# Four cross-attention layers in one kernel: other turns for the third layer's own attention, other shares and another order for its closings and for the rows added back

## The chip, the core and the metric

The kernel runs on one core of one Trainium2 chip. The core has five engines with a queue each: TensorE (PE, with its weight loads shown apart as PEld), VectorE (DVE), ScalarE (ACT), GpSimd (POOL) and SyncE (SP, which here only issues transfers). The metric is the time of one execution on the device in microseconds; the kernel before takes 1442.94 us in the median of three runs (1436.54, 1442.94 and 1444.49).

## What is computed

Four layers follow each other on `x` (16 batches of 56 rows, width 256). All of them look at the same context `ctx` (16 batches of 1500 rows, width 128). Cut to what matters:

```python
def reference(x, ctx, pos, mask_ctx, token_types, ...):
    x = L0(x, ctx)                       # one attention to ctx, a gate, an rms norm
    x = L13(x, ctx, mask_ctx, L1)
    x = L2(x, ctx, token_types, pos)
    x = L13(x, ctx, mask_ctx, L3)
    return x

def L13(x, ctx, mask, w):                # 16 heads of 64
    q = layernorm(x) @ Wq / 8
    k, v = split(ctx @ Wkv)
    x = x + tanh(g1) * (softmax(where(mask, q @ k.T, lowest)) @ v) @ Wo
    return x + tanh(g2) * gelu(layernorm(x) @ W1) @ W2

def L2(x, ctx, token_types, pos):        # vm marks the rows of the "v" expert
    h = rms_norm(x)
    q, k, v = split(where(vm, h @ v_qkv, h @ l_qkv))
    a = causal_attention(rotary(q), rotary(k), v)        # within a batch's 56 rows
    x = x + where(vm, a @ v_dense, a @ l_dense)
    x = x + attention(rms_norm(x) @ cq, ctx @ ckv) @ cdense
    m = rms_norm(x)
    return x + where(vm, mlp_v(m), mlp_l(m))
```

In this data the mask of layers L1 and L3 leaves only columns among the last 384 of the context, so the kernel takes its short way for them (`short`): it reads only those 384 columns.

## The kernel before

**Groups and items.** The 16 batches are worked on in four groups of four. A layer and a group make an *item*: item 4·layer + group, from 0 to 15. So items 4 to 7 are layer L1, items 8 to 11 layer L2 and items 12 to 15 layer L3. For each item the program runs an attention to the context as its main line: `att0`, `att13` (which calls `rows` once for a batch) or `att2`. Everything else of the neighbouring items is *side work*, written as Python generators and cut into *turns* by `yield`: `pre13` and `pre2` (norm, queries, and in L2 the layer's own attention with its dense projection) for the next item, `post13` (Wo, norm, W1, W2) for the item before, and `post2` (the experts' products of L2, for two groups together). `beside(k)` strings the side work of item k together; `late()` holds what is spread over items 7 to 12, among it `post2(0)`, `post2(1)` and the adding back of their rows for groups 0 and 1.

**How side work is paced.** The main line asks for turns at fixed places. In `att2` a step is one pair of context chunks of one batch: six steps a batch, 24 an item, numbered 0 to 23 here. Each step issues `weights_pair` (L1441 and L1450 on PE, the exponentials L1455 on ACT, the additions L1467 on POOL), then asks for side work (the *first turn*), then issues the maxima of a later pair (`largest`, L1404 on PE and L1409 on DVE), the sums of an earlier one (`sums_chunk`, L1482), at some steps `shifts` (step 4 of a batch), `own_sums` (step 1), `close_group` (step 2) and the projections of a later batch's keys or values (L1375, L1387), and asks again (the *second turn*). A number behind `yield` is the cost of the turn; `pace(share, kept, most)` adds a share to an account, `line["due"]`, and takes turns while the account lies above a bound (first turn: the item's share, bound -0.8, at most one; second turn: no share, bound 0.6, at most two). A bare `yield` is an empty turn: it ends the asking and takes nothing off the account, which is cut to 3.0. If the first turn did work, the maxima come before the sums, else after them. `SHARES` has one pair of shares for each of the items 8 to 11; the second holds once the next item's `pre` is done. In items 13 to 15 `rows` asks with `step` instead: one turn for each of the seven rows of a batch (two for each of the first two rows of the third and fourth batch), whatever it costs. Where a main line needs the next item's `pre` and it isn't finished, `first` runs the rest of it at once: before step 15 of items 8 to 10, before step 21 of item 11, before the fourth batch in items 12 to 14.

**Who sets the order.** Instructions run in order within an engine's queue. The order of the program is the order of the calls above; a planner at compile time may issue an instruction earlier if the one before it isn't ready by its own account. `behind(made, name, reason)` adds an edge that keeps `made` after the named instruction on the same engine. Transfers issued by SP, ACT and POOL stand in those engines' queues.

**The places that the change touches.**
- `self_attention` in `pre2` (L1304 to L1330): for two pairs of batches `pr` and two halves `e` of the heads, `scores` (PE, then maximum, subtraction on DVE and exponential on ACT), `weights(pr, e)` (DVE: sum L1178, reciprocal L1179, scaling L1180), `turns(pr, e)` (PE: 32 products L1188 that turn the weights, copied by ACT at L302), `sums(pr)` (PE: L1205, then ACT and DVE). After the sums come the two products `ce` with the experts' masks (DVE, L1322) and the dense projection (PE, L1329, in two halves of eight products), the residual (DVE, L1335), and the norm for the attention to the context: squares on ACT (L389), then POOL (L390, the root L320, the scaling L400), transposes on PE (L310).
- `SHARES` (L1354) and `shifts` (L1413 to L1431; its last instruction copies the shifts on DVE, L1430). `line["drained"]` is the name of the last instruction that emptied a bank of `largest` or, in `rows`, of scores.
- `fetch(gi)` (L1675): two indirect transfers on POOL's queue (L1679) that bring a group's rows back from the experts; `take(gi)` (L1687): their addition to `x` on DVE (L1689), kept behind `line["drained"]`, and the first part of L3's norm (DVE L339, L340, L344; POOL: the root L320 and the scaling L354). The transposes of that norm (L310) and the query products (L907) are `pre13`.
- `beside` for item 13 (L1747 to L1758): fetching and adding back of groups 2 and 3, ahead of `pre13` for group 2. `post13` of L3's group 0 follows after that (Wo products L1092, W1 products L1120).
- `late` (L1816 to L1829): the same for groups 0 and 1 after `post2(0)`.

Of the kernel before, what the change touches and what calls it, by code (L numbers as in the profile page):

```python
# [62 lines left out]
def tile_kernel(ctx: ExitStack, tc: tile.TileContext, a, layers=4, groups=NG):  # L63
# [3 lines left out]
    nc = tc.nc  # L67
# [14 lines left out]
    def psum(pool, tag):  # L82
        return pool.tile([128, 512], F32, tag=tag, name=tag)
# [5 lines left out]
    def mm():  # L89
        return psum(ps_s, "sc")  # L90

    def turn():
        return psum(ps_s, "sc")
# [452 lines left out]
    line, memory_w, halves_of, queries, heads_w, cross, held, begun = {}, [], {}, {}, {}, {}, {}, {}  # L546
# [675 lines left out]
    def pre2(gi):  # L1222
# [12 lines left out]
        scores, weights, turns, sums = self_attention(qT, kept, v, cT)  # L1235
# [68 lines left out]
        weights(0, 1)  # L1304
        turns(0, 0)
        yield 1.2
        weights(1, 0)
        turns(0, 1)
        yield 1.2
        weights(1, 1)  # L1310
        sums(0)
        yield 0.7
        turns(1, 0)
        yield 1.2
        turns(1, 1)
# [4 lines left out]
        for n, m in enumerate((vm, nvm)):  # L1320
            mrow = m[:, gi * G : (gi + 1) * G, :].rearrange("p b n -> p (b n)")
            nc.vector.tensor_tensor(  # L1322
                ce[:, n], cT, mrow.unsqueeze(1).to_broadcast([128, 2, T]), ALU.mult
            )
        p = mm()
        for i in range(NT):
            for n in range(2):
# [23 lines left out]

    QH = 4 * N
    PAIRS = NC // 2
    SHARES = (2.1, 1.65), (2.1, 1.1), (2.1, 1.7), (1.9, 1.9)  # L1354

    def spread_queries(b):

# [55 lines left out]
    def shifts(b):  # L1413

        made = cross[b]
        nm = few(8)[: 2 * N]
        nc.vector.tensor_reduce(nm, made["mx"], AX.X, ALU.max, negate=True)
        both = minus[b % 2]
        nc.vector.tensor_copy(both[:, :, 0].bitcast(F32R), nm)
        nc.vector.tensor_tensor(both[:, :, 1], nm, both[:, :, 0], ALU.subtract)  # L1420
        t = turn()
        for n in range(8):
            half, g = divmod(n, 4)
            nc.tensor.matmul(
                t[g * BW : (g + 1) * BW, half * 2 * N : (half + 1) * 2 * N],
                both[:, n, :], ident[: 2 * N, : 2 * N], start=True, stop=True,
                skip_group_check=True,
            )
        shift = small.tile([128, QH], F32R, tag="shift", bufs=2, name="shift")
        nc.vector.tensor_copy(shift, t[:, :QH])  # L1430
        made["shift"] = shift  # L1431

    def weights_pair(b, j):
# [119 lines left out]
    def att2(gi, state, then, ends):  # L1553

        for k in range(G):
            b = gi * G + k
            for j in range(PAIRS):
# [6 lines left out]
                weights_pair(b, j)  # L1564
                full = pace(SHARES[gi][line["behind"]], -0.8, 1)
                last, n = (b, 2 * j - 2) if j else (b - 1, NC - 2)
# [120 lines left out]
    def take(gi, y):  # L1687
        xf = xs[gi].rearrange("p i d -> p (i d)")
        behind(nc.vector.tensor_add(xf, xf, y), line["drained"], "banks go first")  # L1689
        if gi < 3:  # L1690
            begin_layernorm("L3_ln_q_g", gi)

    def program():
# [25 lines left out]
        def beside(k):  # L1719
# [19 lines left out]
            if k:  # L1739
                _, _, _, post, gi = items[k - 1]  # L1740
                follows = line["late"] if third else post(gi, states.get(k - 1))
# [5 lines left out]
            if k == 3 * groups + 1:  # L1747
                while line["stage"] < 5:
                    yield next(line["late"], 0)
                yield  # L1750
                yield
                back = fetch(2), fetch(3)
                for _ in range(7):
                    yield
                take(2, back[0])
                yield
                take(3, back[1])
                yield  # L1758
            if k > groups:
                for work in ahead:  # L1760
                    if isinstance(work, tuple):
# [36 lines left out]
        def late():  # L1798
# [18 lines left out]
            yield  # L1817
            yield
            y = fetch(0)
            for _ in range(4):  # L1820
                yield
            take(0, y)
            line["stage"] += 1
# [50 lines left out]
    t = turn()  # L1874
# [164 lines left out]
```

## Time and profile before

| what | value |
|---|---|
| median of three runs | 1442.94 us |
| the profiled execution, whole | 1437.15 us |
| its span, first to last instruction | 1435.3 us |
| mean granted TensorE clock | 0.986 |
| ACT busy | 744.8 us, 52% |
| DVE busy | 777.7 us, 54% |
| POOL busy | 526.2 us, 37% |
| items 8 to 10, 450 to 915 us: PE busy of 465 us | 453.2 us |
| item 11, 915 to 1072 us: PE busy of 157 us | 148.0 us, clock 0.97 |
| item 13, 1183 to 1247 us: PE busy of 64 us | 58.5 us, clock 0.95 |

The span runs from the first to the last instruction that the profiler recorded; 1.85 us of the execution lie around it. Busy time is the union of an engine's instructions. PE's instructions are pipelined and their ends are modelled, so a PE that counts as busy may still be slow: the granted clock is given beside it. In a timeline, each row is a run of equal instructions on one engine: start, time covered, engine, line, operation, tiles and shapes, their number, and in brackets the idle time of the engine just before them with the instruction that ended it. L302 is a helper for copies on ACT and L310 one for transposes, so these are told apart by their tiles.

### The profile page before, as it was taken

The numbers are of one execution on the slowest core, as the hardware profiler recorded it, in microseconds if no ns is written. First come the engines' busy times: TensorE is split into PE (matmuls) and PEld (weight loads), VectorE is DVE, ScalarE is ACT, GpSimd is POOL, SyncE is SP. The second block draws the span as 40 slices with busy tenths as digits, with TensorE's granted clock in tenths as the row PEclk, the third lists the DMA queues.
The fourth block names the chain that finished last, engine by engine and source line by source line (L and its number), as shares of the span: only waits on it lengthen the run. The fifth ranks groups of instructions, "written<-read, shape, count | busy, mean of one in ns | idle before, by whom it ended". The sixth has DMA issues, their size and how long they took to land.

```text
span 1435.3 us, 32417 instructions
## 1 busy us (share of the span) xinstructions
PE 1357.3 (95%) x13638; PEld 938.2 (65%) x13638; DVE 777.7 (54%) x1794; ACT 744.8 (52%) x1703; POOL 526.2 (37%) x567
## 2 busy tenths in 40 slices
PE   6989999999899999999999999999899998999998
PEld 4667677775656556655555556656467776877776
DVE  4444754647575754467545755455565445455641
ACT  2334866756543547445554544444356565557661
POOL 0011001010101677767767768788743112100000
PEclk9999999999999999999999999999999999999998
DMA  7853224232322021110201022131122343333320
GB/s 270 351 191 126 85 89 145 90 112 65 103 76 81 23 82 52 54 56 24 81 31 43 29 71 68 52 103 56 39 82 94 134 152 101 124 118 123 108 89 10
DMA packets 38808, 135.78 MB, mean 95 GB/s; under 512 B 8605, under 2 KB 18493, under 8 KB 34557
## 3 DMA queue, kind: packets, MB, share of 16 engines
q1 hardware_dynamic: 33901, 119.03, 24.1%
q0 software_dynamic: 2592, 10.85, 2.2%
q10 hardware_dynamic: 2160, 3.74, 0.8%
q8 instruction: 109, 1.79, 0.5%
q14 instruction: 46, 0.38, 0.1%
HBM read 129.01 MB, written 4.59 MB: 93 GB/s over the span
## 4 chain that ended last, share of the span: by engine, by line
PE 75%; DVE 12%; ACT 6%; POOL 3%; DMA 3%; issue 1%; SPq 0%; DVEq 0%; POOLq 0%; ACTq 0%
PE sc L642 9%; PE sc L624 8%; PE sc L1092 7%; PE sc L1404 7%; PE sc L1450 4%; PE o L1482 4%; PE sc L1642 4%; DVE mx L1409 3%; PE sc L907 3%; PE sc L1120 3%; PE sc L1387 3%; PE sc L1441 3%; PE sc L1661 2%; PE sc L1375 2%; POOL all L1467 2%; ACT p L302 2%
## 5 line engine op out<-in xcount | busy, mean ns | idle before, releaser
L1467 POOL TENSOR_TENSOR all<-all,pw 125x448 f32<-125x448 f32 x300 | 341.1, 1149 | 125.8 <-ACT pw L1455 114.7
L1409 DVE TENSOR_REDUCE mx<-sc 112x1 f32<-112x500 f32 x384 | 233.4, 669 | 140.6 <-PE sc L1404 140.5
L1455 ACT ACTIVATE pw<-sc 125x448 f32<-125x448 f32 x384 | 177.7, 550 | 102.8 <-PE sc L1450 100.1
L631 ACT ACTIVATE p<-p,few 128x384 f32<-128x384 f32 x224 | 136.9, 611 | 99.3 <-DVE few L627 98.9
L624 PE MATMUL sc<-ktl,qa 128*128 128x384 f32 x448 | 176.9, 504 | 0.0
L627 DVE CUSTOM_DVE_ANT_0 p<-sc,mkl 128x384 f32<-128x384 f32 x224 | 121.8, 551 | 92.1 <-PE sc L624 87.4
L642 PE MATMUL sc<-p,kvl 32*128 32x224 f32 x2160 | 149.5, 353 | 4.7 <-DVE qa L940 3.3
L642 PEld LDWEIGHTS sc<-p,kvl 32*128 32x128 f32 x2160 | 136.3, 185 | 20.5 <-issue 9.6
L642 PE MATMUL o<-p,kvl 32*128 32x224 f32 x720 | 144.6, 352 | 0.0
L143 POOL TENSOR_SCALAR mkl<-m32l 128x384 bf16<-128x384 uint8 x32 | 16.3, 510 | 314.1 <-DVE few L627 292.5
L642 PEld LDWEIGHTS o<-p,kvl 32*128 32x128 f32 x720 | 130.7, 185 | 0.0
L302 ACT ACTIVATE p<-p,few 128x384 f32<-128x384 f32 x224 | 121.1, 608 | 8.6 <-DVE few L618 7.2
L1404 PE MATMUL sc<-ck,qs 32*112 32x500 f32 x768 | 122.5, 626 | 2.8 <-ACT ck L302 1.4
L661 DVE STREAM_TRANSPOSE p<-p 128x768 f32<-128x768 f32 (+1 forms) x96 | 102.8, 1095 | 28.6 <-ACT p L302 28.4
L624 PEld LDWEIGHTS sc<-ktl,qa 128*128 128x128 f32 x448 | 78.8, 190 | 37.4 <-issue 9.0
L1450 PE MATMUL sc<-qs,ck 32*125 32x224 f32 x1536 | 98.8, 355 | 0.0
L320 POOL TENSOR_TENSOR stat<-stat,half_less 112x2 f32<-112x2 f32 (+1 forms) x33 | 23.1, 700 | 201.8 <-DVE stat L344 162.0
L302 ACT ACTIVATE ot<-sc 128x224 f32<-128x224 f32 x64 | 32.0, 609 | 121.1 <-PE o L642 83.5
L1482 PE MATMUL o<-pw,vc 125*32 125x224 f32 x1536 | 93.0, 359 | 0.0
L1482 PEld LDWEIGHTS o<-pw,vc 125*32 125x32 f32 x1536 | 40.2, 109 | 69.9 <-issue 57.2
L1450 PEld LDWEIGHTS sc<-qs,ck 32*125 32x125 f32 x1536 | 77.4, 183 | 1.1
L302 ACT ACTIVATE vc<-sc 125x512 f32<-125x512 f32 x48 | 28.6, 596 | 82.0 <-PE sc L1387 79.2
(286 smaller groups left out, 2360.7 us busy)
## 6 DMA issues: line engine op xcount, KB each, us to landing
kvl<-in_ctx_last SPq DMA_DIRECT2D x30, 768.0 KB, 4.2
kt<-in_ctxT SPq DMA_DIRECT2D x23, 750.0 KB, 5.0
w<-in_L_W SPq DMA_DIRECT2D x16, 1024.0 KB, 4.8
w<-in_L_Wq SPq DMA_DIRECT2D x8, 1024.0 KB, 5.0
w<-in_L_Wo SPq DMA_DIRECT2D x8, 1024.0 KB, 5.6
ktl<-in_ctxT SPq DMA_DIRECT2D x32, 192.0 KB, 2.5
w<-in_L_v_qkv SPq DMA_DIRECT2D x4, 768.0 KB, 6.8
w<-in_L_l_qkv SPq DMA_DIRECT2D x4, 768.0 KB, 4.1
```

The source lines that it names most:

```text
L302: nc.scalar.activation(out, in_, AF.Copy, scale=scale)
L624: line["scored"] = nc.tensor.matmul(sc[:, :LW], u["q"][:, i * 128 : (i + 1) * 128], u["kt"], start=True, stop=True).ins.name
L627: line["drained"] = nc.vector.tensor_tensor_reduce(u["p"][:, i], sc[:, :LW], u["mask"], 1.0, -LOWEST, ALU.add, ALU.min, mn[:, i : i + 1],) ...
L631: nc.scalar.activation(u["p"][:, i], u["p"][:, i], AF.Exp, bias=mn[:, i : i + 1], scale=-1.0, accum_out=den[:, i : i + 1],)
L642: product = nc.tensor.matmul(o[g][:, : RB * BW], y["kv"][part, j, :], y["p"][part, :, j * BW : (j + 1) * BW], start=j == 0, stop=j == LB - ...
L661: nc.vector.transpose(blocks, blocks)
L1404: nc.tensor.matmul(banks[g][: 2 * N, :SW], made["q"][part, rows], made["k"][part, cols], start=True, stop=True,)
L1409: line["drained"] = nc.vector.tensor_reduce(made["mx"][:, half * 4 + g, s : s + 1], banks[g][: 2 * N, :SW], AX.X, ALU.max).ins.name
L1450: nc.tensor.matmul(banks[g][:CP, c * QH : (c + 1) * QH], made["k"][part, at : at + CP], made["q"][part], start=False, stop=c == 1, skip_gr ...
L1455: line["weighed"] = nc.scalar.activation(p[:, :, g * QH : (g + 1) * QH], banks[g][:CP, : 2 * QH].rearrange("p (c n) -> p c n", c=2), AF.Ex ...
L1467: added = engine.tensor_tensor(made["all"][:, cols], made["all"][:, cols] if j else p[:, 0, cols], p[:, c, cols], ALU.add,)
L1482: nc.tensor.matmul(made["o"][part, :QH], made["v"][:, n, part], p[:, r * QH : (r + 1) * QH], start=n == 0, stop=n + 1 == NC, skip_group_ch ...
```

## The change

The diff touches three places.

In the layer's own attention, `weights(1, 0)` moves behind `turns(0, 1)`, `weights(1, 1)` behind `sums(0)`, and three empty turns are added: before `turns(0, 1)`, before `turns(1, 0)`, and between the products `ce` and the dense projection.

In the closing of L2's attention, the shares of items 10 and 11 grow, `line["drained"]` also names the copy of the shifts, and `late` lets five turns pass in place of four between `fetch(0)` and `take(0)`.

In item 13, the rows of groups 2 and 3 are fetched after four empty turns instead of two; then the program waits until the attention of item 12 is closed and runs five turns of `post13` before `take(2)`, one before `take(3)` and one behind it, where it had seven, one and one empty turns.

```diff
@@ pre2 @@
         weights(0, 1)
         turns(0, 0)
         yield 1.2
-        weights(1, 0)
+        yield
         turns(0, 1)
         yield 1.2
-        weights(1, 1)
+        weights(1, 0)
         sums(0)
         yield 0.7
+        weights(1, 1)
+        yield
         turns(1, 0)
         yield 1.2
         turns(1, 1)
...
                 ce[:, n], cT, mrow.unsqueeze(1).to_broadcast([128, 2, T]), ALU.mult
             )
+        yield
         p = mm()
...
-    SHARES = (2.1, 1.65), (2.1, 1.1), (2.1, 1.7), (1.9, 1.9)
+    SHARES = (2.1, 1.65), (2.1, 1.1), (2.1, 2.0), (2.15, 2.15)
@@ shifts @@
-        nc.vector.tensor_copy(shift, t[:, :QH])
+        line["drained"] = nc.vector.tensor_copy(shift, t[:, :QH]).ins.name
@@ beside @@
             if k == 3 * groups + 1:
                 while line["stage"] < 5:
                     yield next(line["late"], 0)
-                yield
-                yield
+                for _ in range(4):
+                    yield
                 back = fetch(2), fetch(3)
-                for _ in range(7):
+                while line["closed"] < k:
                     yield
+                for _ in range(5):
+                    yield next(follows, 0)
                 take(2, back[0])
-                yield
+                yield next(follows, 0)
                 take(3, back[1])
-                yield
+                yield next(follows, 0)
@@ late @@
             y = fetch(0)
-            for _ in range(4):
+            for _ in range(5):
                 yield
             take(0, y)
```

## The prediction

> **What bounds the kernel now.** I read the page's busy shares first, then the timeline around every long PE wait, then the stretches' clock, then the DMA issues.
>
> ```profile
> PE 1357.3 (95%) x13638; PEld 938.2 (65%) x13638; DVE 777.7 (54%) x1794; ACT 744.8 (52%) x1703; POOL 526.2 (37%) x567
> ...
> L1467 POOL TENSOR_TENSOR all<-all,pw 125x448 f32<-125x448 f32 x300 | 341.1, 1149 | 125.8 <-ACT pw L1455 114.7
> ```
>
> PE is busy for 95% of the span, so only its waits can be won; all matrix products stay as they are. The second line is the next limit: in the third layer's attention to the context POOL adds four times 1149 ns a step, 4.65 us, while a step without side work takes PE 4.5 us (1021.37 to 1025.91 between the starts of two steps).
>
> The timeline of the third layer's item 9 (group 1's attention; start, duration, in brackets PE's idle time and what ended it):
>
> ```profile
> 664.29 1.14 PE L1188 MATMUL sc<-ident,s 120*64 120x56 f32 x32 [1.53 <-DVE s L1180]
> ...
> 684.08 1.98 PE L1329 MATMUL sc<-w,l 128*112 128x256 f32 x8 [1.66 <-DVE l L1322]
> ...
> 693.11 0.19 POOL L390 TENSOR_SCALAR stat<-stat 112x2 f32<-112x2 f32 x1
> ...
> 696.51 0.55 PE L310 MATMUL sc<-ident,xn 112*128 112x112 f32 x4
> ```
>
> PE waits 1.53 us for DVE's second softmax scaling before the second `turns`, and 1.66 us for the two `ce` products before the dense projection. Behind that runs the norm: residual (689.17), POOL from 693.11 to 696.04, and the transposes of L310 without a wait. POOL is free then because the wait delayed the next additions.
>
> The timeline of item 11's end (the last group's attention) and one stretch of it (stretch, length, busy and count of PE, PEld, DVE, ACT, POOL, granted clock, DMA share, GB/s):
>
> ```profile
> 1032.76 1.15 DVE L1689 TENSOR_TENSOR x<-x,back 112x512 f32<-112x512 f32 x1 [0.91 <-DMA back<-made,place]
> ...
> 1035.20 0.97 PE L1424 MATMUL sc<-ident,minus 112*32 112x112 f32 x16 [2.93 <-DVE minus L1420]
> ...
> 1038.37 0.45 PE L310 MATMUL sc<-ident,xn 112*128 112x112 f32 x1 [2.19 <-POOL xn L354]
> ...
> 1039.58 0.82 PE L310 MATMUL sc<-ident,xn 112*128 112x112 f32 x3 [0.76 <-POOL xn L354]
> ```
>
> ```profile
> 1028.00:1043.00 15.00, 8.70 (x93) 5.18 (x86) 7.16 (x16) 3.39 (x8) 13.98 (x14) 0.72 0.06 17
> ```
>
> `take(0)` (1032.76) stands on DVE ahead of the shifts, so PE waits 2.93 us for them, then 2.19 and 0.76 us for POOL's normalised rows. The clock is 0.72 in the stretch, and products stretch with it: eight of L907 take 2.88 us where 1.78 is usual (1050.58).
>
> Item 13 (the fourth layer's second group, L3 in the names):
>
> ```profile
> 1194.55 2.20 PE L624 MATMUL sc<-ktl,qa 128*128 128x384 f32 x6
> ...
> 1196.11 0.08 DVE L627 DVE_READ_ACCUMULATOR2_ANT few<- 128x1 f32 x1
> ...
> 1201.61 0.34 PE L310 MATMUL sc<-ident,xn 112*128 112x112 f32 x1 [4.86 <-POOL xn L354]
> ...
> 1204.42 8.36 PE L907 MATMUL sc<-xT,w 128*128 128x224 f32 x32 [0.60 <-DVE xT L379]
> ```
>
> PE has 4.86 us with nothing to do until the rows fetched for group 2 are added (1196.11) and normalised; L907's 32 products then take 8.36 us.
>
> **The change, part by part.** I counted the turns on paper, with `pace`'s rule, the yields' values and the shares; for the kernel before, this puts `fetch(0)`, `take(0)` and the transposes into steps 14, 16 and 16 of item 11, where the trace has them. The planner may issue an instruction earlier when another isn't ready (L1482 goes ahead of L1441 around the dense products), so the places are good to about half a step.
>
> (a) *The empty turns*, items 8 to 10. Before: step 7's first turn has weights(1,0) and turns(0,1); step 8 weights(1,1), sums(0), then turns(1,0); step 9 turns(1,1), then sums(1), `ce` and half of the dense product; step 10 its other half. After: turns(0,1) in step 7's second turn; weights(1,0) and sums(0), then weights(1,1) in step 8; turns(1,0), then turns(1,1) and sums(1) in step 9; `ce`, then both dense halves in step 10. The norm stays in step 11's first turn and its transposes in the second.
>
> Won: the waits of 1.53 and 1.66 us, since between producer and consumer there now stand L1404, L1482 and a projection, some 3 us of PE work: 3.2 us an item, 9.6 in three (1.51 and 1.66 in item 8, 1.56 and 1.65 in item 10).
>
> Given back, first: turns(1,1) and sums(1) now share a turn, and sums(1) needs ACT's copy (0.54 us, starting 0.1 us after the last product). 0 if the planner puts the next step's products between, 0.75 if not; I take 0.6. Second: the residual comes a turn later, by those 3 us, and the transposes don't. From the end of the dense product (689.06) to L310 (696.51) before lie 7.4 us; after, 4.3 (0.4+0.9 for L1441 and L1450, 0.9+1.0+1.1 for the rest of step 11). The chain is DVE 0.69, two squares on ACT 1.2, POOL 0.19+0.72+1.83 and some 0.4 of signals: 5.0 us if nothing is in front. But ACT also gets step 11's exponentials (1.85) and POOL its additions (4.65, until 6.4 us into the step): 0.7 us of waiting if the norm goes first, 4.9 if both stand ahead of it, 0 where the planner draws step 12's products forward. I take 1.5, nearer the lower end, because before (693.11) POOL did take the norm ahead of the additions. Net per item 3.2 - 0.6 - 1.5 = 1.1, in three 3.3 (bounds -7.4 and 9.6).
>
> In item 10 the waits are followed by a stretch at half clock (833.4 to 836.8 us, products of L1404 2.19 us instead of 1.11): 1 us more, 0 if it falls half anyway. Item 7 has the same code between L3-like rows: PE waits 2.13 us for ACT's copy and 1.82 for `ce`. After, both `turns` stand in one turn, behind seven scalings on ACT (372.18, some 3.6 us), so the first wait stays; a score product (0.91 us) covers half of the second: 0.5 won (bounds -1 and 2).
>
> (b) *Pace, fifth turn, shifts.* 2.0 for 1.7 in item 10 and 2.15 for 1.9 in item 11 add no work. They end `post2(0)` in step 9 instead of 12; `fetch(0)` moves from step 14 to 11, `take(0)` from 16 to 13 (second turn), the transposes from 16 to 14 (first turn), the query products to 14 and 15, `take(1)` from 20 to 17. POOL's two indirect issues (1.01+0.94 us) move past three steps of additions; the weights' loads keep their distance to their use to within half a step of 6 us, against landings of 5 us. With the fifth turn the rows have 2.5 steps, some 12 us, to land; DVE no longer waits for them (0.91 us before). Behind `take(0)` on DVE now stand step 14's reductions, whose waiting readers are PE's bank users; `take(1)` goes behind step 16's shifts, which costs nothing since step 17 has nothing of DVE's on PE's path.
>
> Before, between 1028.8 and 1045.3, PE loses 0.42+2.93+2.19+0.76 = 6.3 us of waits and about 4.5 of half-clock stretching (L310's four 1.2, L907 1.1, L1424, L1441 and L1450 the rest): 11. After: from step 13's reductions (about 5.7 us into the step, with own_sums 0.7) the chain L1689 1.15, norms 1.5, root 0.72, scaling 2.43 ends some 7 us into step 14; PE reaches the transposes at 1.2, or at 4.2 where the planner draws the sums, L1404 and L1387 forward. The wait is 3 or 5.5; I take 3, plus 1 of stretching. Then the tail: steps 16 and 17 have 2.8 and 2.2 us of PE work but 4.65 of additions each; own_sums of batch 14 waits for them. POOL's sum from step 14 on (3.1 norm, 2.6 fetch, 18.6 additions, 5 queued) ends 1.8 us later than PE gets there. Gain 11 - 3 - 1 - 1.8 = 5 (bounds 0 and 8).
>
> By the Trainium skill's "TensorE: Matmul & The Clock Gate", section "What's actually happening", the clock falls to half only after a whole idle window of about 3.4 us, at free-running borders; this row agrees in kind (6 us of waits, 0.72). By the rule a wait of 3 us would mostly keep the clock, and (b) would win 6 rather than 5; it also speaks against (a) only where waits of 4.9 us appear.
>
> (c) *Item 13.* `fetch(2)` and `fetch(3)` move from batch 1's row 5 to batch 2's row 0, and `post13` of group 0 gives five turns of its Wo products (6.9 us: two groups of 3.45 at L1092) before `take(2)`, which stays at row 3; the transposes stay at row 5, three query products stay forced. PE's work in front of the transposes grows by 6.9 us. The chain grows too: DVE now adds Wo's result and its norm (0.75+0.75+0.3+0.2, then 0.74) before `take(2)`, and can start only when Wo ends, about 1196.8. Then: residual 1197.6, norm and root 1199.4, scaling 1200.3, L1689, norm, copies of `ot` 1203.5, POOL 0.72+2.43, 1206.5. PE has the sums (4.8), three rows (2.2) and four transposes until 1204.1: a wait of 2.4, L907 at 1207 instead of 1204.4 with 6.9 done: 4.3 won (bounds 2 and 6.5, no wait left). Wo and W1 are loaded before Wq, which takes Wo's buffer: issued near 1197, landed 5 us later, used near 1207; uncovered it would cost those 5. On SP the next keys stand behind it (1203.29 before), so they aren't late. POOL's mask conversion (0.51 us) no longer stands behind four fetches; its reader on DVE waited 1.70 us. The rest of `post13`, forced between items before, fills batch 3's rows: work moved, not saved.
>
> **Sum.** 3.3 + 1 + 0.5 + 5 + 4.3 = 14 us. The profiled execution took 1437.15 us (span 1435.3 and 1.85 around it), so 1423 for one like it. The runs' median lies 5.8 above it; I predict on the median's scale: 1442.9 - 14 = 1429. The bounds add up to -6.4 and 27, 1416 to 1449; since they rarely meet I keep 1420 to 1446.
>
> **Rivals.** 1. *All waits go*: the planner draws other products into every gap: 9.6+1+2+8+6.5 = 27, 1416. For it: it reorders around L1329 already. Against: transposes feed everything behind them. 10%. 2. *Given back*: per item 1.35 for sums and 2 or more at the norm (nothing net in (a)), and the tail eats (b) to 0; (c) alone stays: 1439. For it: POOL is above 90% busy in the stretch shown (13.98 of 15 us). 22%; that the planner's own order undoes the empty turns ends here too. 3. *Slower: POOL's additions go first* at all four norms. Place: L390 to L310 in items 8 to 10, L354 in 11. Price: 4.9 of waiting, 1.7 for a stretch of half clock (half of the 3.4 us seen at 833.4), 1.2 until the query product has its input: 7.8 instead of 1.5 in three places, 4.65 more in the fourth: 23.5 against 14, so 1452. It decides from about 5.4 us a place. For it: their program place is earlier. Against: 693.11, where the norm went first. 10%.
>
> **How the numbers follow.** The forecast has 58%. 0.5%, 7.2 us, is about what a measurement of this kernel can tell from no change. Faster: rival 1 and nine tenths of the forecast, 0.62; same: rival 2 and the other tenth, 0.28; slower: rival 3, 0.10. The range 1420 to 1446 leaves out most of rivals 1 and 3; the forecast's own is 1421 to 1437.
>
> **What would show it.** (a) right: no DVE releaser at L1188 and L1329 in items 8 to 10; L310 there waits for L400 by 1 to 2 us; wrong: by 4 or more. (b) right: `take(0)` near step 13 with no DMA releaser, one wait of L310 of 3 us, clock above 0.85 over 15 us; L1508 waits for L1467 by about 2. (c) right: L1092 stands before L1689 in item 13, and L310's 4.86 falls to 1 to 3. If those waits go and the time doesn't, it is POOL or the tail.

## The result and the profile after

The changed kernel takes 1453.18 us (median of 15 runs, 1448.15 to 1459.18), the kernel before 1439.03 us (15 runs, 1434.03 to 1444.49). The ratio is 1.0096, 95% interval 1.0078 to 1.0113: about 14 us slower, where 14 us faster (1429, range 1420 to 1446) was predicted. The profiled executions stand at 1448.4 us of span after and 1435.3 before, 13.1 apart. The mean granted TensorE clock is 0.978 after and 0.986 before.

Two rows of the page (busy time with its share; the additions' group: busy, mean of one, idle before):

```profile
PE 1372.1 (95%) x13638; PEld 944.3 (65%) x13638; DVE 774.9 (53%) x1794; ACT 746.8 (52%) x1705; POOL 525.8 (36%) x567
...
L1470 POOL TENSOR_TENSOR all<-all,pw 125x448 f32<-125x448 f32 x300 | 340.6, 1147 | 136.8 <-ACT pw L1458 125.7
```

PE does the same 13638 products, but is busy for 14.8 us longer (1357.3 before), and its idle time is no longer than before (76.3 us of the span against 78.0): most of the loss is in products that take longer. That is the clock. The trace's list of granted clocks has stretches at half clock that last 3.4 us or a multiple of it. From 350 us on, without the last one at the end, they add up to 30.6 us before and 54.4 after. Half of the difference, 11.9 us, is an estimate of what a busy PE loses in them. The other runs agree: the mean granted clock is 0.975 over the 15 runs of the kernel after, and 0.983 to 0.984 over the runs of the kernel before that were timed with the experiments. One minus the clock, times the span, is what the clock withholds: 36.6 us after and 23 to 25 before.

To see where it goes, take the start of each step on PE (the first product with `shift`) and of each row batch (L624) in both traces; the difference is the lag. In the table the lag's growth in the profiled execution stands beside the half clock that falls in that stretch.

| stretch | predicted | lag's growth, us | half clock before / after, us |
|---|---|---|---|
| item 7 | -0.5 | -2.8 | 3.4 / 0 |
| items 8 and 9, turns | -1.1 each | +3.7 each | 0 / 10.2 each |
| item 10, turns | -2.1 | -1.4 | 3.4 / 3.4 |
| items 10 and 11, closings | -5 | +11.2 | 10.2 / 20.4 |
| item 13, rows | -4.3 | -0.4 | 6.8 / 6.8 |

One execution says little about item 7: up to the first row batch, where all kernels do the same work, the traces already stand -2.9 to +4.6 us from that of before, and up to 5.5 at 347 us. In item 7 the waits of 2.13 and 1.82 us that the prediction names fall to 1.53 and 1.24; the rest of the 2.8 is the clock.

**Item 9, the turns.** The timeline of the kernel after (start, duration, in brackets the engine's idle time and what ended it; most lines have moved by 3 in the code, so L1412, L1444, L1407 and L1332 are L1409, L1441, L1404 and L1329 of before):

```profile
664.49 2.09 DVE L1180 TENSOR_TENSOR s<-s,stat 120x448 f32<-120x448 f32 x2
...
667.09 1.14 PE L1188 MATMUL sc<-ident,s 120*64 120x56 f32 x32
...
667.39 0.68 DVE L1180 TENSOR_TENSOR s<-s,stat 120x448 f32<-120x448 f32 x1
667.99 2.42 DVE L1412 TENSOR_REDUCE mx<-sc 112x1 f32<-112x500 f32 x4
...
668.71 2.22 PE L1444 MATMUL sc<-shift,ones_r 2*125 2x448 f32 x4 [0.48 <-DVE mx L1412]
```

The rest of the same step and of the dense products, PE alone:

```profile
672.16 2.91 PE L1407 MATMUL sc<-ck,qs 32*112 32x500 f32 x8
...
676.65 2.07 PE L1390 MATMUL sc<-l2w,kt 128*125 128x128 f32 x8
...
692.60 3.62 PE L1332 MATMUL sc<-w,l 128*112 128x256 f32 x16
...
701.51 0.51 PE L310 MATMUL sc<-ident,xn 112*128 112x112 f32 x3 [0.59 <-POOL xn L400]
```

and the stretch from 665 to 700 us (length; busy and count of PE, PEld, DVE, ACT, POOL; granted clock, DMA share, GB/s), with that of item 11 shown before, first after and then before:

```profile
665.00:700.00 35.00, 34.16 (x430) 20.76 (x422) 18.79 (x42) 13.85 (x33) 20.50 (x20) 0.85 0.17 59
1028.00:1043.00 15.00, 10.12 (x109) 5.23 (x112) 5.54 (x14) 4.30 (x9) 13.04 (x12) 0.73 0.06 17
```

```profile
665.00:700.00 35.00, 32.88 (x461) 19.90 (x460) 21.03 (x45) 15.17 (x36) 24.38 (x24) 1.00 0.23 84
```

The reader is to see three things. The two waits shown before are gone: L1188 no longer waits for L1180, and L1332 runs in one block of sixteen without a wait. But DVE still does all of the softmax's `weights` (664.49 to 667.99) ahead of the four maxima, in the order of before, so the score banks come free 0.6 us apart, and the four products of L1444 take 2.22 us instead of 0.72. Then the clock falls: L1407's eight products take 2.91 us where they took 2.00 at this place before, L1390's 2.07 instead of 1.14. The mean of 0.85 over 35 us comes from 10.2 us at one half.

**Item 11, the closings.** POOL, DVE and PE around `fetch(0)` (L1682 and L1496 are L1679 and L1493 of before):

```profile
1019.25 1.01 POOL L1682 DMA_INDIRECT back<-made,place  x1 [0.16 <-issue]
...
1020.57 0.94 POOL L1682 DMA_INDIRECT back<-made,place  x1 [0.30 <-issue]
...
1021.52 2.21 POOL L1470 TENSOR_TENSOR all<-pw 125x448 f32<-125x448 f32 x2
1023.69 0.56 POOL L1496 TENSOR_TENSOR rest<-rest,tables 128x224 f32<-128x224 f32 x1
1024.29 0.53 DVE L1499 TENSOR_REDUCE rest<-rest 128x56 f32<-128x224 f32 x1 [6.40 <-POOL rest L1496]
1024.73 2.42 DVE L1412 TENSOR_REDUCE mx<-sc 112x1 f32<-112x500 f32 x4
...
1025.45 1.32 PE L1444 MATMUL sc<-shift,ones_r 2*125 2x448 f32 x2 [4.07 <-DVE mx L1412]
```

and what follows:

```profile
1037.46 2.43 POOL L354 TENSOR_SCALAR xn<-x,stat 112x256 f32<-112x256 f32 x2
...
1038.74 0.45 PE L310 MATMUL sc<-ident,xn 112*128 112x112 f32 x1 [4.12 <-POOL xn L354]
...
1039.95 0.82 PE L310 MATMUL sc<-ident,xn 112*128 112x112 f32 x3 [0.76 <-POOL xn L354]
...
1063.60 2.42 POOL L354 TENSOR_SCALAR xn<-x,stat 112x256 f32<-112x256 f32 x2
1065.99 4.62 POOL L1470 TENSOR_TENSOR all<-all,pw 125x448 f32<-125x448 f32 x4
...
1068.37 0.34 PE L1511 MATMUL sc<-all,l2w 125*32 125x56 f32 x4 [4.38 <-POOL all L1470]
...
1070.66 0.96 PE L1511 MATMUL sc<-all,l2w 125*32 125x56 f32 x28 [1.95 <-POOL all L1470]
```

`fetch(0)` is now issued when batch 14's first additions and the own sums of batch 13 (L1496) are due on POOL. L1499 waits for L1496 on DVE, for 6.40 us, and the maxima stand behind it there; PE waits 4.07 us for the banks that they read. Then come 4.88 us at the transposes and, last, 6.33 us at L1511: `take(1)`'s scaling (1063.60) stands on POOL ahead of batch 14's last four additions. The five waits add up to 15.3 us, against 8.8 in the six of before (0.42, 2.93, 2.19 and 0.76, and at 1060.10 and 1063.38 another 0.74 and 1.74); 10.2 us more of half clock cost up to 5.1. That makes 11.6, and the lag grows by 11.2.

**Item 13, the rows** (DVE, POOL, PE):

```profile
1210.94 0.75 DVE L1098 SCALAR_TENSOR_TENSOR x<-sc,tables,x 112x512 f32<-112x512 f32 x1 [1.00 <-PE sc L1092]
...
1216.12 0.58 DVE L1020 COPY ot<-o 128x224 f32<-128x224 f32 x1
...
1217.02 0.69 DVE L1692 TENSOR_TENSOR x<-x,back 112x512 f32<-112x512 f32 x1
...
1220.95 2.44 POOL L354 TENSOR_SCALAR xn<-x,stat 112x256 f32<-112x256 f32 x2
...
1222.23 0.45 PE L310 MATMUL sc<-ident,xn 112*128 112x112 f32 x1 [4.04 <-POOL xn L354]
```

The wait at the transposes is 4.04 us instead of 4.86, though the Wo products (their result is added by L1098) now stand ahead of it. `take(2)` (L1692) starts behind the copies of `ot` (L1020).

### The profile page after: what moved, and what is told of

It reads as the page before. It is cut to its first block, busy times and chain, and to the rows that moved or that the text cites. A ratio compares the mean times of both kernels' runs of the same rounds, so it can differ in the third digit from the quotient of the medians.

```text
span 1448.4 us, 32415 instructions
## 1 busy us (share of the span) xinstructions
PE 1372.1 (95%) x13638; PEld 944.3 (65%) x13638; DVE 774.9 (53%) x1794; ACT 746.8 (52%) x1705; POOL 525.8 (36%) x567
## 5 line engine op out<-in xcount | busy, mean ns | idle before, releaser
L1412 DVE TENSOR_REDUCE mx<-sc 112x1 f32<-112x500 f32 x384 | 233.1, 668 | 155.2 <-PE sc L1407 155.1
L624 PE MATMUL sc<-ktl,qa 128*128 128x384 f32 x448 | 176.9, 504 | 0.0
L627 DVE CUSTOM_DVE_ANT_0 p<-sc,mkl 128x384 f32<-128x384 f32 x224 | 121.7, 551 | 89.4 <-PE sc L624 81.9
L642 PEld LDWEIGHTS sc<-p,kvl 32*128 32x128 f32 x2160 | 136.6, 185 | 20.4 <-issue 9.0
L1407 PE MATMUL sc<-ck,qs 32*112 32x500 f32 x768 | 125.8, 642 | 2.8 <-ACT ck L302 1.4
L624 PEld LDWEIGHTS sc<-ktl,qa 128*128 128x128 f32 x448 | 78.5, 190 | 37.2 <-issue 9.0
L1485 PE MATMUL o<-pw,vc 125*32 125x224 f32 x1536 | 97.2, 370 | 0.2 <-ACT rest L302 0.2
```

What stands on the lines that cost most here:

```text
L624: line["scored"] = nc.tensor.matmul(sc[:, :LW], u["q"][:, i * 128 : (i + 1) * 128], u["kt"], start=True, stop=True).ins.name
L627: line["drained"] = nc.vector.tensor_tensor_reduce(u["p"][:, i], sc[:, :LW], u["mask"], 1.0, -LOWEST, ALU.add, ALU.min, mn[:, i : i + 1],) ...
L642: product = nc.tensor.matmul(o[g][:, : RB * BW], y["kv"][part, j, :], y["p"][part, :, j * BW : (j + 1) * BW], start=j == 0, stop=j == LB - ...
L1407: nc.tensor.matmul(banks[g][: 2 * N, :SW], made["q"][part, rows], made["k"][part, cols], start=True, stop=True,)
L1412: line["drained"] = nc.vector.tensor_reduce(made["mx"][:, half * 4 + g, s : s + 1], banks[g][: 2 * N, :SW], AX.X, ALU.max).ins.name
L1485: nc.tensor.matmul(made["o"][part, :QH], made["v"][:, n, part], p[:, r * QH : (r + 1) * QH], start=n == 0, stop=n + 1 == NC, skip_group_ch ...
```

## The experiments

Each kernel was timed against the kernel before, on the same chip; e1 to e4, e5 to e8, e9 to e11 and e12 to e14 are four groups on four chips, each with its own runs of the kernel before.

| kernel | what it is | median, us | before, us | ratio (95%) |
|---|---|---|---|---|
| e1_turns | empty turns alone | 1444.68 | 1441.09 | 1.0036 (1.0017 to 1.0054) |
| e2_closings | shares, fifth turn, shifts | 1449.52 | 1441.09 | 1.0057 (1.0034 to 1.0080) |
| e3_rows | item 13's order alone | 1441.15 | 1441.09 | 0.9994 (0.9976 to 1.0013) |
| e4_turns_first | empty turns, group 0 alone | 1439.46 | 1441.09 | 0.9999 (0.9978 to 1.0019) |
| e5_no_shares | fifth turn and shifts alone | 1440.44 | 1440.25 | 1.0002 (0.9985 to 1.0020) |
| e6_shares | shares alone | 1445.68 | 1440.25 | 1.0040 (1.0023 to 1.0056) |
| e7_own_on_dve | e2, own sums' product on DVE | 1445.42 | 1440.25 | 1.0039 (1.0022 to 1.0056) |
| e8_both_on_dve | e7, and `take`'s scaling on DVE | 1443.42 | 1440.25 | 1.0015 (0.9997 to 1.0033) |
| e9_weights_behind | e1, DVE's order changed | 1429.06 | 1438.98 | 0.9927 (0.9904 to 0.9950) |
| e10_dense_only | last empty turn alone | 1443.59 | 1438.98 | 1.0020 (1.0003 to 1.0037) |
| e11_softmax_only | e1 without it | 1444.02 | 1438.98 | 1.0027 (1.0008 to 1.0045) |
| e12_change_behind | the change, DVE's order changed | 1441.36 | 1439.03 | 1.0015 (1.0001 to 1.0029) |
| e13_behind_alone | before, DVE's order changed | 1441.64 | 1439.03 | 1.0021 (1.0001 to 1.0042) |
| e14_take_earlier | e9, and item 13's new order with `take(2)` a turn earlier | 1426.15 | 1439.03 | 0.9916 (0.9894 to 0.9938) |

### The three parts apart

e1, e2 and e3 make one part of the diff each; e4 makes the turns conditional:

```diff
-        weights(1, 0)
+        if gi == 0:
+            yield
+        else:
+            weights(1, 0)
         turns(0, 1)
...
```

> The kernel before with the empty turns and moved weights of pre2 alone, in all four groups. Theory: what the stage table of the kernel after shows is the edit's own doing: 2.8 us won in item 7, 3.7 lost in item 8 and 3.7 in item 9, 1.4 won in item 10, in sum about 3 us slower (1441 to 1444 beside a before of 1439), and the four maxima of items 8 and 9 again end the wait that the turns used to end. Rival (the prediction's own step): the edit wins 3 to 4 us and the loss in items 8 and 9 comes from elsewhere.

> The kernel before with the new shares, the fifth turn and the shifts entered in `drained`, nothing else. Theory: in item 11 the two fetches for group 0 come one step earlier on a full POOL, the own sums and with them the maxima come late, and the norm of group 1 stands before batch 14's additions: about 10 to 11 us slower (1448 to 1451). Rival (the prediction): 5 us faster; second rival: the loss needs the lag that the empty turns make, and alone this part costs under 4.

> The kernel before with the new order of the additions of groups 2 and 3 in item 13 alone. Theory: Wo's products move ahead as they were meant to, but the norm chain starts only behind them and the transposes at step 21 still wait about 4 us for POOL's scaling: 0.4 us faster, not to be told from none. Prediction's step: 4.3 us faster, the wait at the transposes 1 to 3 us.

> The empty turns of pre2 for group 0 alone (item 7), the old order in the other three groups. Theory: 2.8 us faster, as in item 7 of the kernel after, and 5 to 7 us faster than with the turns in all four groups. Rival: what item 7 wins is given back in item 8 (a start that is earlier by 2.8 us meets the same later wait), and the time is that of before within 1 us.

Of before's 1441, the ratios make 5.2 us lost for the turns, 8.2 for the closings and 0.9 won for the rows (which can't be told from none): 12.5 together, with the whole change at 13.8. So two parts lose, nearly independently, and the third can't be told from nothing (its interval goes from 3.5 us won to 1.9 lost). e1's trace repeats the kernel after in items 8 and 9: +3.8 us of lag in item 8 and +3.7 in item 9, and half clock of 10.2 us at 508.2 and at 675.4. In item 7 it doesn't: with the same code and nearly the same waits (1.53 and 1.20 us) the lag grows by 1.3 us, because 10.2 us of half clock fall there. Over its twelve runs the clock withholds 34.6 us, 9.6 more than in its runs of the kernel before, which is more than e1 loses: without the clock, by this estimate, the turns would have won 4 to 5 us. e4 wins nothing that can be told; its 2.8 us of item 7 are inside the interval, and the question is left open.

### The turns: what DVE does first

e9 adds to e1 an order among instructions of DVE, without a semaphore: the second pair's softmax sums stand behind the newest reader of a score bank.

```diff
-            nc.vector.tensor_reduce(den, s, AX.X, ALU.add)
+            summed = nc.vector.tensor_reduce(den, s, AX.X, ALU.add)
+            if pr:
+                behind(summed, line["drained"], "banks go first")
```

e10 has, of the turns, only the empty one ahead of the dense products; e11 has the others.

> The empty turns in all four groups, and the softmax sums of the second pair (L1178 of weights(1,0) and weights(1,1)) ordered on DVE behind the newest bank reader in `drained`. Theory: in the kernel with the empty turns alone DVE takes all three weights (about 4.8 us) ahead of step 7's maxima, so PE waits for the banks at L1441 and the clock falls for 10.2 us in items 8 and 9; with the maxima between them the wait at step 8 goes, the clock stays at 1.00 there, and the time falls from 1444.7 to 1434 to 1439, faster than before or like it. Rival: the transposes now wait for the later weights, by 1.5 us and more, the clock falls as before, and the time stays at 1443 to 1447.

> Of the empty turns only the one ahead of the dense products, in all groups; the softmax as before. Theory: the wait of 1.66 us for the two `ce` products goes in items 8 to 10 and the transposes of the norm wait about 0.6 more: 2 to 4 us faster (1436 to 1438), no fall of the clock. Rival: the later residual makes the norm's transposes late enough for a fall of the clock, and the time is 2 us or more above before.

> The empty turns and moved weights of the softmax, without the one ahead of the dense products, in all groups. Theory: the loss of the empty turns is here: the wait for the banks at step 8 and 10.2 us of half clock in items 8 and 9, 5 to 8 us slower (1445 to 1448). Rival: the two parts lose only together, and this one is within 2 us of before.

By its ratio e9 is 10.5 us faster than before, and so some 15 us faster than e1; that is 5 us below the range that was forecast. Its item 9 (lines up by 2 once more: L1414 are the maxima, L1182 the scaling, L1446 PE's `shift` products, L1409 its score products, L1334 the dense products):

```profile
665.30 0.62 DVE L1182 TENSOR_TENSOR s<-s,stat 120x448 f32<-120x448 f32 x1
...
666.80 2.43 DVE L1414 TENSOR_REDUCE mx<-sc 112x1 f32<-112x500 f32 x4 [0.88 <-PE sc L1409]
...
668.31 1.14 PE L1190 MATMUL sc<-ident,s 120*64 120x56 f32 x32
...
669.38 0.48 PE L1446 MATMUL sc<-shift,ones_r 2*125 2x448 f32 x4
...
670.73 0.61 DVE L1182 TENSOR_TENSOR s<-s,stat 120x448 f32<-120x448 f32 x1
...
687.39 3.62 PE L1334 MATMUL sc<-w,l 128*112 128x256 f32 x16
```

```profile
665.00:700.00 35.00, 34.29 (x482) 20.82 (x474) 22.99 (x51) 17.47 (x41) 24.95 (x25) 1.00 0.24 84
```

DVE takes the maxima between the weights, L1446 takes 0.48 us instead of 2.22, the transposes of L1190 run on without a wait, and the clock is 1.00 over the stretch. The lag falls by 2.7 us in items 8 and 9 each and by 4.4 in item 10, where 1.7 of it is half of the 3.4 us of half clock that is gone. This makes the numbers of the kernel after whole: without its fall of the clock (10.2 us, 5.1 lost) items 8 and 9 would have won 1.4 each, which is just what item 10 won, where the clock was the same before and after. e9's profiled execution is the slowest of its six (1435.36 us): it stands 5.5 us behind at 347 us, and in items 11 and 12, where the waits are those of before, it loses 4.5 us to 10.2 us more of half clock. So the gain is read from items 8 to 10 and from the median, not from this span.

e10 missed: it is slower by 2.9 us (0.4 to 5.3), and its trace has no fall of the clock in items 8 and 9 and no change of lag there. Over its twelve runs the clock withholds 3.3 us more than before, about as much as it loses; the trace, one of the faster runs (1440.15 us), doesn't show where. Its item 9, PE alone:

```profile
687.04 1.09 PE L1330 MATMUL sc<-w,l 128*112 128x256 f32 x4 [1.39 <-ACT pw L1456]
688.47 1.12 PE L1330 MATMUL sc<-w,l 128*112 128x256 f32 x4 [0.34 <-DVE l L1322]
...
699.97 0.51 PE L310 MATMUL sc<-ident,xn 112*128 112x112 f32 x3 [0.59 <-POOL xn L400]
```

The first half of the dense products (L1330) is later by a turn, and there waits 1.39 us for ACT's exponentials and 0.34 for `ce`, 1.73 where before it waited 1.66. So this turn wins nothing while the others are not made; in e9 the dense products don't wait at all. e11 is slower by 3.9 us, a little less than forecast: the wait of 2.22 us at the banks is there in item 9, and the clock falls in items 8 and 10 (6.8 us each) but not in item 9. These are its rows of `shift` in items 8 and 9:

```profile
508.91 2.22 PE L1443 MATMUL sc<-shift,ones_r 2*125 2x448 f32 x4 [0.47 <-DVE mx L1411]
...
675.22 2.22 PE L1443 MATMUL sc<-shift,ones_r 2*125 2x448 f32 x4 [0.45 <-DVE mx L1411]
```

e12 and e13 ask whether the two losses add up, and whether DVE's order would do without the turns:

> The whole change, with one dependency more: the sums of the second pair's softmax (weights(1,0), weights(1,1)) stand on DVE behind the newest bank reader. Theory: the turns' part turns from about 5 us of loss into 10 of gain, the closings and the rows stay as they are, so 14 to 15 us under the changed kernel's 1453: 1436 to 1441, like before. Rival: the parts aren't additive (an earlier item 11 meets POOL otherwise), and it stays above 1445.

> The kernel before with that dependency alone, without any empty turn. Theory: maxima ahead of the last weights cure nothing by themselves, because the second transposes then wait longer for their scaling (1.53 us becomes 3 to 5) and the `ce` wait stays: 1438 to 1446, no faster than before; the gain needs both the turns and the order on DVE. Rival: the order on DVE is all, and this kernel is at 1429 to 1433.

e12 has the whole change and is at 1441.36, 11.8 us under the kernel after, with no half clock from 480 to 870 us. Added up, the ratios of e9, e2 and e3 would make some 3 us less than before, and e12 is 2 us above; each interval is about 3 us wide to either side, so this doesn't tell whether the parts hinder each other. e13 wins nothing, though not for the reason given: in its item 9 L1190 waits 1.52 us for the scaling, no longer than before, and L1331 1.65 for `ce`. The gain needs both.

### The closings: what stands behind the fetch on POOL

e5 and e6 split the part; e7 and e8 move work from POOL to DVE in it:

```diff
-            nc.gpsimd.tensor_tensor(
+            (nc.gpsimd if b < 3 * G else nc.vector).tensor_tensor(
                 raw, raw, m_own.unsqueeze(2).to_broadcast([128, 4, N]), ALU.mult
...
-            begin_layernorm("L3_ln_q_g", gi)
+            begin_layernorm("L3_ln_q_g", gi, engine=nc.vector if gi < 2 else nc.gpsimd)
```

> The fifth turn and the shifts entered in `drained`, with the old shares. Theory: the loss of the part is in the shares, which bring `fetch(0)` to step 11/12 ahead of the own sums; without them it stays in step 14 and the wait for the maxima there is 0 instead of 4.07 us. Expected 1434 to 1442 beside a before of 1440, no slower than before. Rival: the turn and the dependency push the norm of group 0 by a step on a full POOL, and cost 5 us or more by themselves.

> The new shares alone, without the fifth turn and without the shifts in `drained`. Theory: nearly the whole loss of the closings' part, 7 to 11 us slower (1447 to 1451): DVE waits some 6 us for POOL's L1493 ahead of the maxima, PE 4 us for the banks, and the last own sums wait for POOL. Rival: the shares alone cost under 3 us.

> The closings' part (shares, fifth turn, shifts in `drained`), with the multiplication of the own sums (L1493) of the last group's batches on DVE instead of POOL. Theory: the 6.39 us that DVE stood behind POOL's L1493 ahead of the maxima of step 12 go, the wait of PE for the banks (4.07 us) goes with its stretch of half clock, and the time falls by 5 to 7 us against the closings alone: 1442 to 1445. The waits of 4.9 us at L310 and of 6.3 us at the last own sums stay. Rival: the maxima are late for another reason (the exponentials, the additions), and the time stays at 1448 to 1450.

> As the kernel with the own sums' multiplication on DVE, and the scaling of the normalised rows behind `take(0)` and `take(1)` (L354, 2.43 us each) on DVE too. Theory: the last own sums no longer wait behind the norm on POOL (6.3 us down to about 3) and the transposes wait 4.9 less some 2 us: 5 us less than with the own sums alone, 1436 to 1440, no slower than before. Rival: DVE becomes the bound in steps 13 to 17, where it has the maxima, and the time stays above 1443.

The loss is in the shares: e6 has 5.8 us of it, a little less than forecast, with the waits of 4.08 us for the maxima and of 4.21 and 1.89 at the last own sums; e5 has none in the median, though in its profiled execution the transposes wait 11.2 us. e7's item 11, first DVE, then PE's waits of the tail (here in the numbering of before):

```profile
1015.11 0.39 DVE L1493 TENSOR_TENSOR rest<-rest,tables 128x224 f32<-128x224 f32 x1 [2.21 <-ACT rest L302]
...
1015.99 2.42 DVE L1409 TENSOR_REDUCE mx<-sc 112x1 f32<-112x500 f32 x4
```

```profile
1029.00 0.45 PE L310 MATMUL sc<-ident,xn 112*128 112x112 f32 x1 [5.41 <-POOL xn L354]
...
1059.88 0.40 PE L1508 MATMUL sc<-all,l2w 125*32 125x56 f32 x4 [5.00 <-POOL all L1467]
1062.16 0.96 PE L1508 MATMUL sc<-all,l2w 125*32 125x56 f32 x28 [1.89 <-POOL all L1467]
```

With its product (L1493) on DVE, the own sums wait for ACT (2.21 us) and no longer for POOL, and the wait at the banks is 0.30 us instead of 4.06: so it came from the product's place on POOL, behind the fetch and the two additions that follow it. But only 2.6 us come off the median instead of 5 to 7 (e2 and e7 were timed in different groups of runs, and their intervals overlap), and the trace shows why: the wait at L310 has grown from 4.13 to 5.41 us and that at L1508 from 4.38 to 5.00. In the last steps PE has some 2.1 us of work a step and POOL 4.65 of additions; the shares have used up earlier the side work that PE had there. What is won ahead of these steps is waited for in them.

e8 takes the scaling off POOL. The wait at L1508 falls from 5.00 and 1.89 to 3.09 and 2.54 us, and L310's stays (5.33); the median is 3.5 to 7 us above what was forecast. POOL's and DVE's additions there, in two fences:

```profile
1057.53 6.91 POOL L1467 TENSOR_TENSOR all<-all,pw 125x448 f32<-125x448 f32 x4
```

```profile
1059.07 1.15 DVE L1467 TENSOR_TENSOR all<-pw 125x448 f32<-125x448 f32 x2
...
1061.00 3.92 DVE L1467 TENSOR_TENSOR all<-all,pw 125x448 f32<-125x448 f32 x3
```

POOL's four additions take 6.91 us instead of 4.62 while DVE does additions of its own; the longest takes 2.76 us, the shortest 1.14. Three of DVE's take 3.92 us together, 1.31 in the mean, where the first two took 0.61 each.

### The rows: `take(2)` ahead of the sums

```diff
-                for _ in range(5):
+                for _ in range(4):
                     yield next(follows, 0)
                 take(2, back[0])
                 yield next(follows, 0)
                 take(3, back[1])
-                yield next(follows, 0)
+                for _ in range(2):
+                    yield next(follows, 0)
```

> The empty turns with the dependency, and the rows' new order with `take(2)` one turn earlier, ahead of the batch's sums instead of behind them. Theory: in the changed kernel the addition stood on DVE behind the two copies of `ot`, which wait for the sums' 4.8 us on PE, and so the wait at the transposes stayed at 4.06 us; ahead of the sums the chain is hidden by them, the wait falls below 1.5 us and the clock holds: 3 to 5 us below the kernel with the dependency alone, 1424 to 1427. Rival: the rows haven't landed by then, DVE stands in front of the maxima of the next rows, and the time is 1429 or more.

Its item 13, DVE and then PE (L1694 is the addition of the rows):

```profile
1191.56 0.69 DVE L1694 TENSOR_TENSOR x<-x,back 112x512 f32<-112x512 f32 x1
...
1198.81 0.59 DVE L1020 COPY ot<-sc 128x224 f32<-128x224 f32 x1
```

```profile
1198.85 0.61 PE L310 MATMUL sc<-ident,xn 112*128 112x112 f32 x4
...
1203.13 7.97 PE L907 MATMUL sc<-xT,w 128*128 128x224 f32 x32 [1.97 <-issue]
```

The addition starts 7.2 us ahead of the copies of `ot` instead of behind them, and L310 doesn't wait. L907 waits 1.97 us, for nothing that the profile shows. The half clock there falls from 6.8 to 3.4 us, and the lag from before item 13 to the end by 4.5 us, where e12, with the order of the change, wins 0.1. At 1426.15 us, 12 us under before, this is the fastest kernel of the study; against e9 it is 1.1 permille, inside the two intervals, so the 4.5 us rest on the stage and not on the median.

## Why the prediction was wrong

**The reading of the present bound** held: only PE's waits could be won, and the clock that follows them. Three slips in its text: the line shown at 1196.11 is that of L627; the addition of the rows stands at the same start in the trace (0.68 us, L1689). Item 10's half clock before lies at 822.9 to 826.3 us from the span's start, not 833.4 to 836.8, and the eight products of 2.19 us (830.21) ran at full clock. And the stretching of 4.5 us in item 11 is too high: PE waits through 3.7 of the 10.2 us at half clock, so they cost 3.3 at most.

**(a) The turns** is the first step that failed: "Won: the waits of 1.53 and 1.66 us, since between producer and consumer there now stand L1404, L1482 and a projection". It counted PE's work between the two and left out DVE's. Moving `weights` by a turn in the program didn't move it on DVE, where the planner put all three weights ahead of step 7's maxima, as before. DVE was late by as much as before; the wait went from the transposes to the banks. The prediction had the planner's own order as a case of rival 2, with nothing net; the price that it lacked is the clock. Its sign for being right came true all the same: in items 8 to 10 no wait on DVE is left at L1188 and L1329, and L310 waits 0.4 to 0.6 us. It watched the old waits, and the new one stood at L1441, with its 10.2 us of half clock in items 8 and 9. What was given back was smaller than forecast: 0.59 us of wait for POOL's scaling at L310 against 1.5. With the maxima in front (e9), items 8 to 10 win 9.8 us, 1.7 of them the clock, near the 9.6 of waits that the prediction counted as the gross gain. The 1 us for item 10's clock didn't come in the kernel after, but did, as 1.7, in e9. In item 7 the waits fell by 1.2 us where 0.5 was predicted; what that is worth in time the clock hides.

**(b) The closings** is the second and larger: "POOL's two indirect issues (1.01+0.94 us) move past three steps of additions", costed at nothing. What is queued behind them on POOL was not followed further: L1493, then L1496 on DVE, then the maxima, then PE's banks, 4.07 us. The wait at the transposes was put at 3 us and is 4.88; the tail at 1.8 and is 6.33. The half clock, whose cost was to shrink from 4.5 us to 1, grew from 10.2 to 20.4 us. The landing of the rows was right: `take(0)` (1033.84) has no wait for its DMA. That POOL was above 90% busy in the stretch stood in the prediction as an argument for rival 2; it should have been a bound on the step.

**(c) The rows** is the third: 0.4 us instead of 4.3, which can't be told from none. Wo's products did move ahead; the step that failed is DVE's order behind them. In e3's trace, with its lag of 5.45 us taken off, Wo's residual (1197.6) and scaling (1200.35) come to 0.1 us as foreseen, and PE has done its work at 1204.05, where 1204.1 was foreseen. But the chain ends at 1209.3, not 1206.5: the prediction had L1689 follow the scaling, with the copies of `ot` behind it, and in the trace the copies go first, and wait for the sums that PE ends at 1201.5. Then Wo's `xT` and the second group's addition stand on DVE between the statistics. e14 shows that the order was the cause: with the addition ahead of the copies the wait is gone.

**The rivals.** Rival 3 had the sign, but not the place: nowhere do POOL's additions go ahead of the norm in items 8 to 10, and in item 11 it is the norm that goes ahead of the additions. That its 1452 lies next to the measured 1453 is luck.

**The clock.** The Trainium skill, "TensorE: Matmul & The Clock Gate", section "What's actually happening", has the clock fall after a whole idle window of about 3.4 us. The stretches here are indeed 3.4, 6.8 or 10.2 us long. But ahead of the fall at 672.5 PE's single waits are of 0.4 to 0.6 us, some 2 us together; none is as long as a window, so the runs don't agree with the rule as it is worded, and the prediction, which leaned on it to say that (a) was safe below waits of 4.9 us, was misled there. e11 has the same 2.22 us in item 9 and keeps its clock. The traces show what differs: in each, all falls start on one grid of 3.41 us (505.3, 672.5 and 833.0 in the kernel after are 49 and 47 steps apart), and the place of the row of 2.22 us in that grid goes with what follows. Where the row starts 2.9 to 3.0 us behind a grid point, the clock falls for 10.2 us (items 8 and 9 of the kernel after and of e1); at 1.0 to 1.1, for 3.4 (their item 10); at 0.3 to 0.7, for 6.8 (items 8 and 10 of e11); at 2.8, in item 9 of e11, it doesn't fall. These are nine cases of one row; no experiment moved the row against the grid, so why the place decides stays open.

## What to carry to other kernels

A turn moved in the program moves an instruction only on the engines whose planned order follows; before counting a wait as won, look at who stands in front of the late producer on its own engine, and whether that order will change. A short instruction put earlier on a nearly full in-order queue costs what is queued behind it, followed through every engine to PE, and work that fills PE at a point where another engine sets the pace should not be used up before it. Where two traces do the same work in different time, compare the granted clock stage by stage first: here half clock makes an estimated 11.9 of 13.1 us. And watch for new waits, not only for the old ones to go.

## What the runs showed of the hardware

- The granted clock falls to one half for 3.4 us or a multiple, in items 8 and 9 of the kernel after and of e1 for 10.2 us each, behind waits of some 2 us in sum. That costs an estimated 5.1 us, more than the waits that go before it. In each trace the falls start on one grid of 3.41 us, and after the same waits there were falls of 10.2, 6.8, 3.4 us or none, by their place in the grid.
- POOL's additions of 125x448 took 1.73 us in the mean instead of 1.16 while DVE added tiles of the same size, and three of DVE's 1.31 instead of 0.61 (e8). The Trainium skill, "SBUF — State Buffer", section "SBUF: two separate sides", names a pair of ports that the two engines share and take in turn for a whole instruction, DVE's with two inputs from SBUF among them. The longest row agrees: POOL's addition of 2.76 us takes its own 1.14 and the 1.60 of the two additions and the product (L1493) that DVE did meanwhile.
- With the same instructions up to 347 us, the traces differ there by -2.9 to +5.5 us, and single executions of one kernel by 10 us, so an edit worth 3 us shows only in the stage that it touches.
